# Two graph layers on one core: which PSUM banks the second layer's sums and the loaded rows' transposes use

## The chip, the cores and the metric

The kernel runs on one core of one Trainium2 chip. The metric is the device time of one execution in microseconds (us). The kernel before ran three times: 755.61, 748.73 and 752.56 us, a median of 752.56 us. One more execution was taken with the hardware profiler; it has a time and a span of its own, given below.

## The reference

There are N = 4096 nodes with D = 64 features, and a dense 4096 x 4096 adjacency matrix of zeros and ones in float32, in which a row has some eight ones on average. Two layers follow each other, both on a layer-normed and rectified input, both with a residual.

```python
# layer 0: mean over neighbours of the logarithm map on the Poincare ball
h = jnp.maximum(_layernorm(x, axis=-1), 0.0)
w = adj / jnp.maximum(adj.sum(axis=1, keepdims=True), 1e-08)
log_ij = _logmap(h[:, None, :], h[None, :, :], c)
agg = jnp.einsum('ij,ijc->ic', w, log_ij)
x = x + _expmap(0, agg @ L0_weight + L0_bias, c)
# layer 1: a row's neighbours weighted by their rank from the row's end
h = jnp.maximum(_layernorm(x, axis=-1), 0.0)
support = h @ L1_weight
rank = jnp.cumsum(mask, axis=1)
k = jnp.minimum(rank[:, -1:], 100.0)
pos = rank - (rank[:, -1:] - k)
w = mask * jnp.where(pos > 0, 0.5 ** (k - pos), 0.0)
x = x + w @ support + L1_bias
```

Layer 0 needs, for each node, the rows of its neighbours and a nonlinear function of each pair. Layer 1 is a product of a 4096 x 4096 matrix of powers of two with a 4096 x 64 matrix.

## The kernel before, in words

All is in `tile_gnn_kernel` (L549 to L1569). The nodes are cut into 32 row blocks of 128 rows; eight row blocks form a quarter, so there are four quarters, each with a mask in SBUF.

**Loads (L873 to L897).** A row block is read in two halves of 1 MB each, into one of three slots of `room`; each half is two transfers of 512 KB, issued by the sync engine SP (L879). `load(rb, h, n)` is called 128 times, n = 0 and n = 1 for each half. A call takes one PSUM bank, transposes eight 128 x 128 blocks into it on TensorE (PE, L888), and copies the bank into the quarter's mask with one instruction on ScalarE (ACT, L891). The slot is free for the next transfer when its transposes are done.

**Lists (L899 to L1130).** `pack` (PE, L917) multiplies the mask by codes, so that a row's ones become 256 words in a bank of the pool `ps_w`; `fetch_words` (ACT) copies them out, and `search` (VectorE, DVE, L981 and L983) finds the largest ones. From these come six neighbours for every row, and, per quarter, a list of the rows that have more (the tail: `tail_split`, `tail_first`, `tail_second`, whose searches are L1093 and L1095).

**Units (L1132 to L1298).** Layer 0's pairs are worked off in 17 units, numbered 0 to 16: units 0 to 15 take two row blocks each (12 gathers), units 5 to 16 have a part of the tail besides, or alone (6 or 9 gathers). `gather` (GpSimd, POOL, L1139) fetches neighbours' rows with an indirect transfer each, 288 in all. `tail_rows` prepares the tail's own rows (ACT L1156, L1163, L1170; PE L1169 and L1178), `differ` and `weigh` compute the pair's function (DVE and ACT, L1192 to L1251; L1222, L1234, L1241 and L1246 are among them), and `total` adds up: by DVE for the six, and for the tail by ACT (L1261) and PE (L1266). The gathers' buffers are two, so the gathers of unit k + 2 wait for the weights of unit k (L1234).

**The middle (L1305 to L1406).** In five groups of row blocks (8, 8, 8, 6 and 2), `middle` finishes layer 0 and makes the operand `sup` of layer 1: transposes into a bank of `ps_o` (`transposed`, L1300 to L1303), products into a bank of `ps_w` (L1333 to L1348), layer norm, and in its last stage products into `ps_t` (L1384 to L1394) and the split into three bf16 parts side by side, 192 columns (L1403, L1405).

**Layer 1's sums (L1414 to L1447).** `step` (DVE, L1412) turns a mask into layer 1's powers of two. The sum over the 32 operand blocks is cut into four parts of 16, 7, 6 and 3 blocks. `collect(c, p, n)` handles part c for two row blocks of quarter p (n = 0 to 3), so there are 64 calls: it takes one PSUM bank, fills it by matmuls (PE, L1422, 1024 in all, and L1430, 32 in the last part), and adds the bank to the result `acc`. 24 of the calls (part 0, and part 3 for n < 2) do that on DVE (L1441, L1445). The other 40 copy the bank out with ACT (L1436) into a buffer, "dg" for odd n and "mr" for even n, of which there is one each, and POOL adds the buffer's three parts to `acc` (L1438). The buffer "mr" is also what the tail's L1261 writes and L1266 reads. `write` (SP, L1451) sends finished rows out, and a flag (L1558 to L1567) ends the program.

**Who sets the order.** The functions are put in a list with the time at which each ought to run (`at`, L1454 to L1555), which becomes a priority. A scheduler then orders each engine's instructions by priority and by a timeline of its own, in which a tile has to wait until its pool has a buffer free. So the number of banks that a pool offers enters into the order written for every engine.

**The PSUM pools (L836 to L841)** hold eight banks together: `ps_a` two, `ps_w` two, and `ps_t`, `ps_o`, `ps_s` and `ps_m` one each. Before the change both `load` and `collect` take their banks from `ps_a`; `ps_w` serves `pack` and the middle's products, `ps_o` the middle's transposes.

Of the kernel before, what the change touches and what calls it, by code (L numbers as in the profile page):

```python
# [11 lines left out]
F32 = mybir.dt.float32  # L12
BF16 = mybir.dt.bfloat16
# [6 lines left out]
P = 128  # L20
# [28 lines left out]
QB = 8  # L49
# [499 lines left out]
def kernel(  # L549
# [66 lines left out]
    with ExitStack() as fast:  # L616
# [174 lines left out]
        late = masks[NQ - 1].bitcast(F32).rearrange("p b c -> p (b c)")  # L791
# [44 lines left out]
        ps_a = fast.enter_context(tc.tile_pool(name="ps_a", bufs=2, space=PSUM))  # L836
        ps_w = fast.enter_context(tc.tile_pool(name="ps_w", bufs=2, space=PSUM))
        ps_t = fast.enter_context(tc.tile_pool(name="ps_t", bufs=1, space=PSUM))
        ps_o = fast.enter_context(tc.tile_pool(name="ps_o", bufs=1, space=PSUM))
# [4 lines left out]
        st = {}  # L844
# [3 lines left out]
        sums = [(0, 16, (0, 1)), (16, 7, (2,)), (23, 6, (3,)), (29, 3, (4,))]  # L848
# [6 lines left out]
        sup, o = [], 0  # L855
        for c, (_, nb, _) in enumerate(sums):
            n = nb + (c == len(sums) - 1)
# [15 lines left out]
        def load(rb, h, n):  # L873

            k = (NH * rb + h) % LD
            a_sb = room[:, k * HC : (k + 1) * HC]
            if n == 0:
                for m in range(2):
                    nc.sync.dma_start(  # L879
                        out=a_sb[:, bass.ts(m, HC // 2)],  # L880
                        in_=adj_v[rb // JH, rb % JH, :, h * HC + m * HC // 2 : h * HC + (m + 1) * HC // 2],
                    )
            a_ps = ps_a.tile([P, QB, P], BF16, name="a_ps")

            upper = a_sb.bitcast(BF16)
            for k in range(QB):
                e = 2 * (QB * n + k) + 1
                nc.tensor.transpose(a_ps[:, k, :], upper[:, e : 2 * HC : 2 * JH], ident_b)  # L888
            q, b = divmod(rb, QB)
            j0 = h * JH + n * QB  # L890
            nc.scalar.activation(  # L891
                masks[q][:, j0 : j0 + QB, bass.ts(b, P)],
                a_ps,
                AF.Copy,
                scale=2.0**-ONE,
                saturate=False,
            )  # L897
# [515 lines left out]

        def collect(c, p, n):  # L1414

            pool = 0 < c < len(sums) - 1 or (c == len(sums) - 1 and n >= 2)
            b0, nb, _ = sums[c]
            end = c == len(sums) - 1
            o = ps_a.tile([P, 2, 2 * P], F32, name="a_ps")
            for k in range(2):  # L1420
                for j in range(nb):
                    nc.tensor.matmul(  # L1422
                        o[:, k, 0:W3],
                        lhsT=masks[p][:, b0 + j, bass.ts(2 * n + k, P)],
                        rhs=sup[c][:, j, :],
                        start=(j == 0),
                        stop=(j == nb - 1 and not end),
                    )
                if end:
                    nc.tensor.matmul(  # L1430
                        o[:, k, 0:W3], lhsT=last, rhs=sup[c][:, nb, :], start=False, stop=True
                    )
            ab = acc[:, p * QB + 2 * n : p * QB + 2 * n + 2, :]
            if pool:
                ev = (lst if n % 2 else blk).tile([P, 2, W3], F32, name="dg" if n % 2 else "mr")
                nc.scalar.activation(ev, o[:, :, 0:W3], AF.Copy, scale=2.0**-W8_SHIFT)  # L1436
                for k in range(3):
                    nc.gpsimd.tensor_tensor(ab, ab, ev[:, :, k * D : k * D + D], ALU.add)  # L1438
                return
            red = lst.tile([P, 2, D], F32, name="wsb")  # L1440
            nc.vector.tensor_reduce(  # L1441
                red, o[:, :, 0:W3].rearrange("p k (n c) -> p k c n", n=3), AX.X, ALU.add
            )
            a = ab.rearrange("p k c -> p (k c)")
            nc.vector.scalar_tensor_tensor(  # L1445
                a, red.rearrange("p k c -> p (k c)"), 2.0**-W8_SHIFT, a, ALU.mult, ALU.add
            )  # L1447
# [18 lines left out]
        for rb in range(NB):  # L1466
            for n in range(4):
                t = T0 + TLOAD * (rb + n / 4)
                at(t, load, rb, n // 2, n % 2)
                at(t + TLOAD / 4 * 1.3, pack, rb, n // 2, n % 2)  # L1470
            at(loaded(rb) + 1.0, fetch_words, rb)
            at(loaded(rb) + 2.0, search, rb)
            if rb % 2:
                at(loaded(rb) + 5.5, counts, rb - 1)
                at(loaded(rb) + 8.0, seeds, rb - 1)
                nl = 2 if rb < QB else 4
                if (rb + 1) % nl == 0:
                    at(loaded(rb) + 5.0, ell_lists, rb + 1 - nl, nl)
# [62 lines left out]
        for when, c, p in pairs:  # L1541
            t = max(t, when + 20.0)
            left[p] -= 1
            for n in range(QB // 2):
                at(t, collect, c, p, n)
                t += max(1.0, 0.2 * sums[c][1])
                if left[p] == 0 and n % 2:
                    at(t, write, p, n // 2)
# [43 lines left out]
```

## Time and profile before

| what | value |
|---|---|
| three runs | 755.61, 748.73, 752.56 us, median 752.56 us |
| profiled execution, its own time | 754.09 us |
| its span | 752.2 us |
| mean granted TensorE clock | 0.668 |
| PE busy | 400.0 us (53%) |
| DVE busy | 403.2 us (54%) |
| POOL busy | 350.5 us (47%) |
| ACT busy | 345.6 us (46%) |
| adjacency transfers (q1) | 72.93 MB, 26.9% of the time of 16 DMA engines |

The span is the profiled part of the execution; 1.9 us of its time lie outside. The profiled execution took 1.5 us more than the median of the runs.

The profile page names an instruction by its line, engine and operation, then its output and input tiles with buffer numbers left out, and a count. In a group's row the first pair of numbers is the total busy time and the mean length in ns of one instruction; the next is the idle time of that engine just before these instructions and the releaser that ended most of it. A timeline row begins with the start and the length in us and ends with the idle time ahead and its releaser. The releaser "issue" means that the profile shows nothing that the engine waited for, and "remote" that the event came from somewhere the trace does not name. In a table of windows each row gives the length of the window, then busy time and, in brackets, number of instructions of PE, PE's weight loads, DVE, ACT and POOL, then the granted clock, the busy share of the DMA engines and GB/s.

### The profile page before, as it was taken

The numbers are of one execution on the slowest core, as the hardware profiler recorded it, in microseconds if no ns is written. First come the engines' busy times: TensorE is split into PE (matmuls) and PEld (weight loads), VectorE is DVE, ScalarE is ACT, GpSimd is POOL, SyncE is SP. The second block draws the span as 40 slices with busy tenths as digits, with TensorE's granted clock in tenths as the row PEclk, the third lists the DMA queues.
The fourth block names the chain that finished last, engine by engine and source line by source line (L and its number), as shares of the span: only waits on it lengthen the run. The fifth ranks groups of instructions, "written<-read, shape, count | busy, mean of one in ns | idle before, by whom it ended". The sixth has DMA issues, their size and how long they took to land.

```text
span 752.2 us, 11841 instructions
## 1 busy us (share of the span) xinstructions
PE 400.0 (53%) x4094; PEld 344.2 (46%) x4094; DVE 403.2 (54%) x1557; ACT 345.6 (46%) x791; POOL 350.5 (47%) x423
## 2 busy tenths in 40 slices
PE   3742465643632628636067351452274378979881
PEld 3542353532531517535054241342164168979871
DVE  7742386734880518927169463793623136764520
ACT  6742465733842529836156251343242214565430
POOL 1374606246475440562705454587274713007892
PEclk9865576755855757855556555555556669988997
DMA  8994567755963536956201111221111110000001
GB/s 310 384 323 137 192 217 245 261 168 154 343 198 94 180 95 217 322 164 191 33 17 17 29 34 23 44 38 26 30 27 33 28 15 13 14 10 1 2 22 40
DMA packets 42858, 88.23 MB, mean 117 GB/s; under 512 B 14756, under 2 KB 20388, under 8 KB 42660
## 3 DMA queue, kind: packets, MB, share of 16 engines
q1 hardware_dynamic: 21458, 72.93, 26.9%
q0 software_dynamic: 9504, 10.67, 8.1%
q10 hardware_dynamic: 11826, 3.78, 2.3%
q8 instruction: 34, 0.56, 0.3%
q14 instruction: 36, 0.29, 0.1%
HBM read 83.11 MB, written 4.24 MB: 116 GB/s over the span
## 4 chain that ended last, share of the span: by engine, by line
DVE 23%; another core or an unknown queue 22%; PE 20%; ACT 16%; issue 10%; DMA 5%; ACTq 2%; POOL 1%; DVEq 0%; SPq 0%; POOLq 0%
PE a_ps L1422 9%; ACT mask L891 7%; PE a_ps L888 3%; DVE mask L1412 3%; PE words L917 2%; DMA room<-in_adj 2%; DVE cand L981 1%; DVE tl L1095 1%; DVE tb L1093 1%; ACT oh L1156 1%; PE sel L1266 1%; POOL acc L1438 1%; DVE wsb L983 1%; DMA w_sb<-in_L_gnn_weight 1%
## 5 line engine op out<-in xcount | busy, mean ns | idle before, releaser
L1139 POOL DMA_INDIRECT g<-tab_d,ell_i x192 | 198.0, 1031 | 266.2 <-DVE d L1234 84.7
L891 ACT ACTIVATE mask<-a_ps 128x1024 fp8e5<-128x1024 bf16 x128 | 128.2, 1028 | 113.8 <-remote 84.6
L888 PE MATMUL a_ps<-ident_b,room 128*128 128x128 bf16 x1024 | 107.4, 272 | 63.6 <-ACT mask L891 37.4
L1422 PE MATMUL a_ps<-room,mask 128*128 128x192 bf16 x1024 | 109.1, 260 | 32.5 <-issue 25.9
L888 PEld LDWEIGHTS <-room 128*128 128x128 bf16 x1024 | 92.9, 158 | 69.9 <-issue 68.0
L1139 POOL DMA_INDIRECT g<-tab_d,tail_i x96 | 93.8, 977 | 50.8 <-issue 28.1
L1422 PEld LDWEIGHTS <-mask 128*128 128x128 fp8e5 x1024 | 93.1, 104 | 41.1 <-issue 39.3
L917 PEld LDWEIGHTS <-mask 128*128 128x128 fp8e5 x1024 | 49.5, 115 | 107.6 <-ACT mask L891 56.7
L917 PE MATMUL words<-pk,mask 128*128 128x64 bf16 x1024 | 61.1, 219 | 70.2 <-ACT mask L891 44.4
L981 DVE MAX8 cand<-wsb 128x8 f32<-128x256 f32 x96 | 40.5, 422 | 88.5 <-ACT wsb L928 80.8
L1266 PE MATMUL sel<-d,mr 128*128 128x65 f32 x192 | 41.3, 379 | 20.2 <-issue 16.7
L1266 PEld LDWEIGHTS sel<-d,mr 128*128 128x128 f32 x192 | 39.0, 295 | 24.9 <-issue 19.6
L1438 POOL TENSOR_TENSOR acc<-acc,dg 128x128 f32<-128x128 f32 x60 | 28.2, 469 | 36.0 <-ACT dg L1436 33.9
L1412 DVE TENSOR_TENSOR mask<-mask 128x1024 int16<-128x1024 int16 x60 | 40.7, 678 | 6.6 <-ACT q__5085 L1241 4.0
L1441 DVE TENSOR_REDUCE wsb<-a_ps 128x128 f32<-128x384 f32 x24 | 13.3, 555 | 46.0 <-remote 27.8
L1261 ACT ACTIVATE mr<-oh,r 128x128 f32<-128x128 bf16 x96 | 29.3, 389 | 18.0 <-DVE acc L1445 7.5
L1438 POOL TENSOR_TENSOR acc<-acc,mr 128x128 f32<-128x128 f32 x60 | 28.5, 475 | 14.6 <-ACT mr L1436 12.7
L1169 PE MATMUL mi<-ident_b,oh 128*128 128x128 bf16 x96 | 12.6, 283 | 38.1 <-ACT oh L1163 28.2
L904 PE MATMUL words<-gn,ones_b 1*128 1x352 bf16 x32 | 12.3, 390 | 35.1 <-ACT cn L931 20.9
L1156 ACT ACTIVATE oh<-row,tail_r 128x128 bf16<-128x128 bf16 x96 | 29.4, 389 | 3.2 <-DVE tail_r L1109 3.1
L1169 PEld LDWEIGHTS <-oh 128*128 128x128 bf16 x96 | 8.9, 128 | 41.1 <-ACT oh L1163 29.2
L1170 ACT COPY mr<-mi 128x768 bf16<-128x768 bf16 (+1 forms) x20 | 13.5, 674 | 30.6 <-PE mi L1169 12.2
(332 smaller groups left out, 775.1 us busy)
## 6 DMA issues: line engine op xcount, KB each, us to landing
room<-in_adj SPq DMA_DIRECT2D x128, 512.0 KB
g<-tab_d,ell_i POOLq DMA_INDIRECT x192
hp_d<-mask SPq DMA_DIRECT2D x1, 1560.0 KB
g<-tab_d,tail_i POOLq DMA_INDIRECT x96
mr<-hp_d ACTq DMA_DIRECT2D x8, 146.2 KB
tab_d<-mask POOLq DMA_DIRECT2D x2, 520.0 KB
hi<-tab_d ACTq DMA_DIRECT2D x16, 65.0 KB
mask<-in_x SPq DMA_DIRECT2D x2, 512.0 KB
```

What stands on the lines that cost most here:

```text
L888: nc.tensor.transpose(a_ps[:, k, :], upper[:, e : 2 * HC : 2 * JH], ident_b)
L891: nc.scalar.activation(masks[q][:, j0 : j0 + QB, bass.ts(b, P)], a_ps, AF.Copy, scale=2.0**-ONE, saturate=False,)
L917: nc.tensor.matmul(w, lhsT=masks[q][:, j, bass.ts(b, P)], rhs=pk, start=False, stop=True, skip_group_check=True,)
L981: nc.vector.max(out=top, in_=src)
L1139: nc.gpsimd.indirect_dma_start(out=g[:, k, :], out_offset=None, in_=tab_d, in_offset=bass.IndirectOffsetOnAxis(ap=i, axis=0),)
L1156: nc.scalar.activation(oh[:, k, :], row128, AF.Abs, bias=tail_r[:, t0 + k // TB, k % TB : k % TB + 1], scale=-1.0,)
L1169: nc.tensor.transpose(mp[:, k - k0, :], oh[:, k, :], ident_b)
L1261: nc.scalar.activation(mr[:, k, :], u["oh"][:, k, :], AF.Copy, scale=r[:, e2 + k : e2 + k + 1])
L1266: nc.tensor.matmul(ag[:, k // TB, :], lhsT=mr[:, k, :], rhs=d[:, e2 + k, :], start=(k % TB == 0), stop=(k % TB == TB - 1),)
L1412: nc.vector.tensor_tensor(m[:, :, j, :], m[:, :, j, :], m[:, :, j - 1 if j else JH - 1, :], ALU.add)
L1422: nc.tensor.matmul(o[:, k, 0:W3], lhsT=masks[p][:, b0 + j, bass.ts(2 * n + k, P)], rhs=sup[c][:, j, :], start=(j == 0), stop=(j == nb - 1 ...
L1438: nc.gpsimd.tensor_tensor(ab, ab, ev[:, :, k * D : k * D + D], ALU.add)
```

## The change

Two functions change where their PSUM bank comes from. In `load`, every third call takes the bank of `ps_o` in place of one of `ps_a`: 86 calls take `ps_a` and 42 take `ps_o`. In `collect`, calls with odd n take a bank of `ps_w` and calls with even n one of `ps_a`. The local name `pool` of `collect` becomes `late`. The pools themselves stay as they are. No instruction is added or removed, but the order in which the scheduler writes them changes on every engine but SP.

```diff
@@ load
-            a_ps = ps_a.tile([P, QB, P], BF16, name="a_ps")
+            pool, name = (ps_a, "a_ps") if st.setdefault("loads", 0) % 3 < 2 else (ps_o, "o")
+            st["loads"] += 1
+            a_ps = pool.tile([P, QB, P], BF16, name=name)
@@ collect
-            pool = 0 < c < len(sums) - 1 or (c == len(sums) - 1 and n >= 2)
+            late = 0 < c < len(sums) - 1 or (c == len(sums) - 1 and n >= 2)
             b0, nb, _ = sums[c]
             end = c == len(sums) - 1
-            o = ps_a.tile([P, 2, 2 * P], F32, name="a_ps")
+            pool, name = (ps_w, "words") if n % 2 else (ps_a, "a_ps")
+            o = pool.tile([P, 2, 2 * P], F32, name=name)
@@ collect, further down
-            if pool:
+            if late:
                 ev = (lst if n % 2 else blk).tile([P, 2, W3], F32, name="dg" if n % 2 else "mr")
```

## The prediction

> **What bounds the kernel now.** I read the page first (shares, groups), then POOL's waits, the timelines of POOL and PE, and windows over the last 150 us. No engine is busy over 54% of the span, so the bound differs by stage. The dearest groups of the page (busy, mean ns, idle ahead and what ended it):
> ```profile
> L1139 POOL DMA_INDIRECT g<-tab_d,ell_i x192 | 198.0, 1031 | 266.2 <-DVE d L1234 84.7
> L891 ACT ACTIVATE mask<-a_ps 128x1024 fp8e5<-128x1024 bf16 x128 | 128.2, 1028 | 113.8 <-remote 84.6
> L888 PE MATMUL a_ps<-ident_b,room 128*128 128x128 bf16 x1024 | 107.4, 272 | 63.6 <-ACT mask L891 37.4
> L1139 POOL DMA_INDIRECT g<-tab_d,tail_i x96 | 93.8, 977 | 50.8 <-issue 28.1
> ```
> The 288 gathers, at some 1.25 us each with their gap, fill about 360 us of POOL between 33 and 634 us; the rest of that stretch POOL waits, mostly for a unit's weights (L1234) two units back. So up to 634 us the path runs from a unit's weights through the next gathers, with loads sharing ACT, PE and the transfer queue. After it POOL has only the L1438 additions, and its timeline shows them late and then dense (start, length):
> ```profile
> 633.14 0.95 POOL L1139 DMA_INDIRECT g<-tab_d,tail_i  x1 [0.30 <-issue]
> 666.70 1.52 POOL L1438 TENSOR_TENSOR acc<-acc,dg 128x128 f32<-128x128 f32 x3 [32.60 <-ACT dg L1436]
> 678.05 1.83 POOL L1438 TENSOR_TENSOR acc<-acc,mr 128x128 f32<-128x128 f32 x3 [9.84 <-ACT mr L1436]
> 680.48 1.72 POOL L1438 TENSOR_TENSOR acc<-acc,mr 128x128 f32<-128x128 f32 x2 [0.60 <-ACT mr L1436]
> 682.16 0.45 POOL L1438 TENSOR_TENSOR acc<-acc,dg 128x128 f32<-128x128 f32 x1
> ```
> From 682 to 739 us POOL hardly pauses, and 13 us of output follow. The windows (PE busy comes first, POOL's fifth) say who is full before and after that point:
> ```profile
> 634.00:648.00 14.00, 13.30 (x146) 12.55 (x145) 12.46 (x43) 9.19 (x26) 0.09 (x1) 0.88 0.08 19
> 648.00:662.00 14.00, 14.00 (x155) 13.39 (x151) 10.44 (x31) 8.66 (x28) 0.00 (x0) 1.00 0.01 2
> 662.00:678.00 16.00, 11.23 (x110) 10.37 (x109) 9.12 (x51) 9.95 (x32) 1.36 (x3) 0.85 0.04 11
> 678.00:694.00 16.00, 15.95 (x149) 15.03 (x148) 7.57 (x18) 7.64 (x19) 13.76 (x29) 0.83 0.01 2
> ```
> PE is full until 662 us, then POOL and PE both have a hole until 678 us. There PE's next sum waits for a bank whose evacuation (L1436) stands behind the last unit's chain on ACT, because the evacuation into "mr" needs the buffer which the unit's L1266 frees at 677.5 us. A third view, PE's timeline while POOL gathers, shows single matmuls that wait for nothing the profile names:
> ```profile
> 597.34 0.32 PE L1422 MATMUL a_ps<-room,mask 128*128 128x192 bf16 x1 [1.79 <-issue]
> 599.46 0.32 PE L1422 MATMUL a_ps<-room,mask 128*128 128x192 bf16 x1 [1.80 <-issue]
> 601.57 0.32 PE L1422 MATMUL a_ps<-room,mask 128*128 128x192 bf16 x1 [1.79 <-issue]
> ```
> More banks cannot help a PE that crawls like this. ACT likewise stood still for 20.4 us up to 277.1 us, inside a gather.
>
> **What the Trainium skill says.** "Perfetto Trace Analysis", Optimization Strategy: consistent bubbles can mean too little SBUF or PSUM for the next tile. The trace agrees only in the stretch 662 to 678 us; before it PE has no bubble, after it POOL is the busy one. "PSUM — Partial Sum Buffer", Specifications (TRN2): eight banks to a partition, and GpSimd reaches none. That is this kernel's shape: its pools hold all eight banks, and each late sum needs a copy by ACT (0.49 us) before POOL adds. The same page, Engine vs sequencer instructions: the queues of ScalarE, VectorE and GpSimd are strict FIFO. The trace agrees: the evacuations at 677.5 us stand behind L1261 at 674.2 us. So a bank freed later by ACT order is not cured by one more bank. "Perfetto Trace Analysis", DMA Instruction — SWDGE (GPSIMD): the row ends when descriptors are written, not when data landed; so the 0.95 us of a gather is POOL's own work, which no bank shortens.
>
> **The change part by part.** No instruction is added or removed: 1024 transposes (L888), 1024 matmuls (L1422), 128 mask copies, 40 evacuations and 120 additions stay. Of the 128 loads, 42 now use the bank "o", which the middle's own transposes (L1302) use too; of the 64 sums 32 use the two "words" banks, which L917 (packing) and L1345 (middle) use. What is moved is the order that the scheduler writes out, because it models banks; I compared the two programs engine by engine.
>
> *The tail.* In the new program the sums with odd n of the second group (six of them) stand ahead of the last unit's chain on ACT and PE, and all go through the buffer "dg". Each costs 0.49 us (copy) and about 1.5 us (three additions) in series, near 2.0 us; the hole of 9.84 us takes five. At 682.3 us POOL would have seven tiles done where it had 3.3: 3.7 tiles at 1.42 us (what a tile with alternating buffers takes in the dense stretch) is 5.2 us gained. What is late next: those same buffers. The rest of the group now ends in a run of five "mr" tiles and has one more "mr" pair, five pairs in one buffer, where an addition waits for a copy of 0.49 us plus hand-over, about 0.6 us each (the 0.60 in the timeline): 3.0 us lost. The dense stretch has 3.7 us of small gaps that end with an evacuation; with four banks about 1.5 us of it goes. Sum: -5.2 + 3.0 - 1.5 = -3.7 us. Bounds: 0 (the six evacuations each wait for POOL, and L1241, L1246 and L1261 of the last unit queue behind them on ACT, so the unit ends later) and -7. The last sums' operands are ready 8 to 10 us before they are used, so this much fits.
>
> *The middle of the units.* In the new program seven pairs of tail searches (L1093, L1095) stand on DVE ahead of unit 11's weights, and on PE 43 more matmuls of the first group (65 for 22), and their wait for a words bank, ahead of unit 13's tail rows (L1169). Gather 13 began without a wait at 507.1 us; unit 11's weights were at 500.95 us, so 6 us were spare. Seven pairs are about 6 us of DVE plus a transfer's round trip; two evacuations of the first group (L1441, 0.56 us each) now stand ahead of unit 13's weights, the gate of gather 15. With half of the 6 us hidden in the slack I take +3 us. Bounds 0 and +7.
>
> *The loads.* A third bank lets PE transpose one more load while ACT stalls. The scheduler used it to pull loads forward: ahead of unit 5's L1222 on ACT stand 99 mask copies for 90, of unit 6's 118 for 105, from unit 8 on 128 for 128. Each is 1.03 us of ACT and 0.5 MB of transfer, 1.5 us at the 346 GB/s seen from 307 to 324 us. That work has to be done anyway; in before, 11 of these 13 ran in the shadow of gather 8. If the new order only fills earlier holes (ACT idles 113.8 us ahead of L891) nothing is lost; I take +1 us. Bounds -10 and +17.
>
> Sum against the profiled execution (754.1 us: span 752.2, about 1.9 around it): -3.7 + 3 + 1 = +0.3 us. The profiled execution lies 1.5 us above the median of the runs; carried over to the median of 752.6 this is 752.9 us.
>
> **The rivals.** *Likeliest: about the same, 752.9 us* (746 to 758). For: after 678 us POOL limits, before 662 us PE is full, and the gathers' length is untouched.
>
> *Faster, 743 us.* The third bank really is what loads lack: PE waits 37.4 us at L888 for L891, and SP's load transfers wait 118.5 us for L888. At each of some eight ACT stalls one more half slot is freed, 8 x 1.5 = 12 us of transfer; half on the path, 6, and the tail's 3.7: -9.7 us. Against: behind the transposes the mask still needs ACT, and the longest stall, 15.5 us, would still be there one load later.
>
> *Slower, 763 us.* One mechanism: unit 6's weights, the gate of gather 8 at 307.3 us, are put behind 13 more loads (17 us), and gather 8 then runs with nothing left to hide. If half of it is not won back later (8 us) and the middle costs its upper 7 us, less the tail's 3.7: +11. It decides from the point where gather 8 starts over 8 us later and the last gather (634 us) does too.
>
> *No effect on the banks' waits, 757 us.* The words banks are held by the middle's L1345 until its copy L1353, so PE stands at the fourth sum of the first group ahead of unit 13's tail rows: +4 us with the tail's gain used up by the last unit's later chain.
>
> **How the numbers follow.** Likeliest 0.36, faster 0.21, slower 0.35, the last 0.08. About 1% is what a measurement here can tell from no change, so 745 to 760 us is "same": the likeliest and the last, 0.44 in all, faster 0.20, slower 0.36, the edges of the cases trading a point. The range reaches over the middle of both outer cases: 743 less 2 for a tail of its full -7, 741; 763 plus 5 for more of the 17 us not won back, 768. The faster case beyond 741 and the slower one beyond 768 leave out about 0.2.
>
> **What would show it.** Tail right: five "dg" additions between 668 and 678 us, and POOL dense to the end some 4 us earlier counted from the last gather; wrong: the last unit's L1261 later by as much. Middle: gather 13 with a wait ahead of it, ended by DVE L1234. Loads: start of gather 8 against 307.3 us, and ACT's wait at L891. The forecast is wrong if the last gather ends more than 8 us away from 634 us in either direction, since nothing behind it makes that good.

## The result, and the profile after

The changed kernel took 785.3 us (780.81 to 788.81, four runs) against 752.69 us before (the three runs and a fourth of 752.83 us): 1.043 of before, 95% interval 1.036 to 1.051, or 32.6 us more. The forecast was 752.9 us, its upper end 768.

The run of the changed kernel that was profiled has a span of 782.7 us, 30.5 us longer. In the changed source the lines after `load` stand two further down, those after `collect` three (L1141 was L1139, L1236 was L1234, L1441 was L1438). The same groups on its page:

```profile
L1141 POOL DMA_INDIRECT g<-tab_d,ell_i x192 | 193.7, 1009 | 304.4 <-DVE d L1236 94.3
L893 ACT ACTIVATE mask<-a_ps 128x1024 fp8e5<-128x1024 bf16 x86 | 86.8, 1034 | 95.0 <-remote 71.4
...
L1141 POOL DMA_INDIRECT g<-tab_d,tail_i x96 | 91.9, 958 | 50.3 <-issue 27.7
...
L890 PE MATMUL a_ps<-ident_b,room 128*128 128x128 bf16 x688 | 71.7, 272 | 30.1 <-ACT mask L893 10.5
```

A gather still costs 1.0 us; PE's wait for a transposing bank fell as intended, from 37.4 to 10.5 us for the two banks of `ps_a`. But the idle time ahead of the neighbours' gathers rose from 266.2 to 304.4 us. POOL's timeline at the end, to be laid beside that of before, whose last addition is the first line here:

```profile
738.00 0.98 POOL L1438 TENSOR_TENSOR acc<-acc,dg 128x128 f32<-128x128 f32 x2
```
```profile
664.96 0.95 POOL L1141 DMA_INDIRECT g<-tab_d,tail_i  x1 [0.31 <-issue]
697.97 2.13 POOL L1441 TENSOR_TENSOR acc<-acc,dg 128x128 f32<-128x128 f32 x3 [32.07 <-ACT dg L1439]
700.70 1.53 POOL L1441 TENSOR_TENSOR acc<-acc,dg 128x128 f32<-128x128 f32 x3 [0.60 <-ACT dg L1439]
702.83 1.54 POOL L1441 TENSOR_TENSOR acc<-acc,dg 128x128 f32<-128x128 f32 x3 [0.60 <-ACT dg L1439]
...
725.54 1.58 POOL L1441 TENSOR_TENSOR acc<-acc,mr 128x128 f32<-128x128 f32 x3 [1.04 <-ACT mr L1439]
729.52 1.52 POOL L1441 TENSOR_TENSOR acc<-acc,mr 128x128 f32<-128x128 f32 x3 [2.40 <-ACT mr L1439]
732.98 1.53 POOL L1441 TENSOR_TENSOR acc<-acc,mr 128x128 f32<-128x128 f32 x3 [1.94 <-ACT mr L1439]
736.76 0.99 POOL L1441 TENSOR_TENSOR acc<-acc,dg 128x128 f32<-128x128 f32 x2 [2.25 <-ACT dg L1439]
...
769.30 0.99 POOL L1441 TENSOR_TENSOR acc<-acc,mr 128x128 f32<-128x128 f32 x2
```

The last gather starts at 664.96 instead of 633.14 us, 31.8 us later. The hole of 9.84 us is filled with "dg" tiles as forecast, and what was won there is lost again further on, mostly in the run of "mr" tiles. From the first addition to the end of the last (770.28 us here, 738.98 before) both kernels take 72.3 us. So the whole loss lies ahead of the last gather. Where, is read from the starts of the gathers (us, from the two timelines of POOL):

| gathers of unit | 3 | 4 | 5 | 6 | 7 | 8 | 10 | 12 | 13 | 14 | 16 |
|---|---|---|---|---|---|---|---|---|---|---|---|
| before | 116.7 | 145.8 | 170.5 | 197.2 | 251.5 | 307.3 | 401.6 | 476.3 | 507.1 | 543.3 | 626.8 |
| after | 119.5 | 151.3 | 180.6 | 214.3 | 277.6 | 331.6 | 424.4 | 503.7 | 540.3 | 572.9 | 658.7 |
| later by | 2.8 | 5.5 | 10.1 | 17.1 | 26.1 | 24.3 | 22.8 | 27.4 | 33.2 | 29.6 | 31.9 |

26.1 us are lost by unit 7. The gathers of units 5, 6 and 7 wait for the weights of units 3, 4 and 5, so 20.6 us of them (26.1 less 5.5) are lost while units 3 to 5 are worked off. Only 3.3 us are won back by unit 10, and from there to unit 16 another 9.1 us are lost, 5.8 of them at unit 13. Four timelines of the changed kernel show the dearest piece, between unit 6's gathers and unit 7's; first ACT, then PE, then DVE, then POOL:

```profile
223.44 1.15 ACT L1165 ACTIVATE oh<-oh 128x1152 bf16<-128x1152 bf16 x1
229.25 1.02 ACT L893 ACTIVATE mask<-o 128x1024 fp8e5<-128x1024 bf16 x1 [4.65 <-remote]
241.86 1.02 ACT L893 ACTIVATE mask<-a_ps 128x1024 fp8e5<-128x1024 bf16 x1 [11.60 <-remote]
255.89 0.80 ACT L1172 COPY mr<-mi 128x768 bf16<-128x768 bf16 x1 [13.00 <-remote]
...
274.36 1.35 ACT L1224 ACTIVATE g<-d 128x1344 f32<-128x1344 f32 x1
```
```profile
230.32 1.01 PE L890 MATMUL o<-ident_b,room 128*128 128x128 bf16 x8 [3.99 <-issue]
256.74 0.48 PE L1171 MATMUL mi<-ident_b,oh 128*128 128x128 bf16 x3 [25.41 <-ACT mr L1172]
...
259.71 0.70 PE L1180 MATMUL mi<-mr 128*128 128x65 bf16 x9
```
```profile
261.34 0.43 DVE L983 MAX8 cand<-wsb 128x8 f32<-128x256 f32 x1 [21.13 <-ACT wsb L930]
...
271.57 0.35 DVE L1210 TENSOR_TENSOR d<-g,mi 128x192 f32<-128x192 f32 x1
```
```profile
277.56 0.94 POOL L1141 DMA_INDIRECT g<-tab_d,ell_i  x1 [24.98 <-DVE u L1237]
```

The same places in the kernel before:

```profile
241.81 1.02 ACT L891 ACTIVATE mask<-a_ps 128x1024 fp8e5<-128x1024 bf16 x1 [6.23 <-remote]
...
248.34 1.32 ACT L1222 ACTIVATE g<-d 128x1344 f32<-128x1344 f32 x1
```
```profile
243.31 0.68 PE L1178 MATMUL mi<-mr 128*128 128x65 bf16 x9 [1.25 <-ACT mr L1170]
```
```profile
246.81 0.34 DVE L1208 TENSOR_TENSOR d<-g,mi 128x192 f32<-128x192 f32 x1
```
```profile
251.52 0.95 POOL L1139 DMA_INDIRECT g<-tab_d,ell_i  x1 [12.96 <-DVE u L1235]
```

While POOL gathers (up to 252.6 us), ACT does one instruction in some 12 us and PE waits for it. In both kernels ACT runs freely again 3.3 us after the gathers' end, at 255.89 us here and at 241.81 us before. From there to unit 5's L1224 it needs 18.5 us, with eleven mask copies of loads on the way; before, to L1222, it needed 6.5 us, with four. The copies do not hold L1224 by themselves. L1224 squares what DVE's L1210 writes, and L1210's last input comes from PE's L1180, which had ended at 260.4 us. But L1210 ran only at 271.57 us, 11.2 us later, since nine searches (L983), with the rest of the list work of loads pulled ahead, are written in front of it on DVE; before, it ran 2.8 us after its input, behind three searches. That is 8.4 of the 12.0 us. The copies are in it too, since the first of the nine waits for words that ACT copies out behind some of them (L930, 5.0 us after ACT runs freely, where before it was 1.3 us). So unit 5's weights, and with them the gathers of unit 7, wait for loads and their lists that the scheduler now puts ahead.

Why is this not won back later, when fewer loads are left? The windows from unit 8's gathers to unit 9's, first before, then after (PE, weight loads, DVE, ACT, POOL, clock, DMA share, GB/s):

```profile
307.30:335.50 28.20, 14.82 (x135) 13.44 (x133) 15.70 (x52) 16.66 (x33) 22.09 (x21) 0.63 0.74 256
335.50:350.70 15.20, 6.90 (x73) 6.48 (x72) 12.18 (x51) 9.88 (x15) 0.04 (x2) 0.61 0.66 218
```
```profile
331.60:358.80 27.20, 9.80 (x66) 8.96 (x66) 12.04 (x55) 13.13 (x28) 21.04 (x21) 0.52 0.44 136
358.80:374.60 15.80, 2.98 (x37) 2.28 (x38) 11.92 (x49) 3.51 (x8) 0.00 (x0) 0.50 0.11 19
```

ACT has 16.6 us of work here in place of 26.5, PE 12.8 in place of 21.7, and the stretch is as long as before: 43.0 us for 43.4. In its first part POOL gathers; in its second DVE is the fullest engine and has as much to do as before, 11.9 us for 12.2. The loads were free in it. Moved ahead of units 3 to 6, they are paid for.

### The profile page after: what moved, and what is told of

It reads as the page before. It is cut to its first block, busy times and chain, and to the rows that moved or that the text cites. A ratio compares the mean times of both kernels' runs of the same rounds, so it can differ in the third digit from the quotient of the medians.

```text
span 782.7 us, 11824 instructions
## 1 busy us (share of the span) xinstructions
PE 407.9 (52%) x4094; PEld 347.3 (44%) x4094; DVE 409.7 (52%) x1557; ACT 344.2 (44%) x791; POOL 344.4 (44%) x423
## 4 chain that ended last, share of the span: by engine, by line
another core or an unknown queue 26%; DVE 23%; PE 18%; ACT 12%; issue 8%; DMA 5%; POOL 4%; ACTq 1%; SPq 0%; DVEq 0%; POOLq 0%
ACT mask L893 5%; POOL acc L1441 4%; PE words L1425 4%; PE a_ps L1425 4%; DVE mask L1414 4%; DMA room<-in_adj 3%; PE a_ps L890 2%; DVE tl L1097 2%; DVE tb L1095 2%; DVE cand L983 1%; PE sel L1268 1%; PE o L890 1%; DMA w_sb<-in_L_gnn_weight 1%; ACT mr L1263 1%
## 5 line engine op out<-in xcount | busy, mean ns | idle before, releaser
L1141 POOL DMA_INDIRECT g<-tab_d,ell_i x192 | 193.7, 1009 | 304.4 <-DVE d L1236 94.3
L893 ACT ACTIVATE mask<-a_ps 128x1024 fp8e5<-128x1024 bf16 x86 | 86.8, 1034 | 95.0 <-remote 71.4
L1425 PEld LDWEIGHTS <-mask 128*128 128x128 fp8e5 x1024 | 96.8, 107 | 50.1 <-issue 47.1
L890 PEld LDWEIGHTS <-room 128*128 128x128 bf16 x1024 | 91.3, 158 | 52.9 <-issue 52.6
L1141 POOL DMA_INDIRECT g<-tab_d,tail_i x96 | 91.9, 958 | 50.3 <-issue 27.7
L919 PEld LDWEIGHTS <-mask 128*128 128x128 fp8e5 x1024 | 48.3, 114 | 119.3 <-ACT mask L893 59.9
L983 DVE MAX8 cand<-wsb 128x8 f32<-128x256 f32 x96 | 40.2, 419 | 110.2 <-ACT wsb L930 88.9
L890 PE MATMUL a_ps<-ident_b,room 128*128 128x128 bf16 x688 | 71.7, 272 | 30.1 <-ACT mask L893 10.5
L1425 PE MATMUL a_ps<-room,mask 128*128 128x192 bf16 x512 | 62.4, 271 | 17.8 <-issue 14.5
L1425 PE MATMUL words<-room,mask 128*128 128x192 bf16 x512 | 60.9, 264 | 20.2 <-issue 17.4
L1268 PE MATMUL sel<-d,mr 128*128 128x65 f32 x192 | 38.5, 364 | 40.6 <-issue 21.3
L1268 PEld LDWEIGHTS sel<-d,mr 128*128 128x128 f32 x192 | 36.7, 283 | 42.7 <-issue 22.9
L893 ACT ACTIVATE mask<-o 128x1024 fp8e5<-128x1024 bf16 x42 | 43.5, 1035 | 16.7 <-remote 11.8
L1441 POOL TENSOR_TENSOR acc<-acc,dg 128x128 f32<-128x128 f32 x60 | 28.6, 477 | 41.0 <-ACT dg L1439 38.2
L890 PE MATMUL o<-ident_b,room 128*128 128x128 bf16 x336 | 37.6, 266 | 14.4 <-issue 11.1
L906 PE MATMUL words<-gn,ones_b 1*128 1x352 bf16 x32 | 12.1, 383 | 43.7 <-ACT cn L933 40.2
```

The lines of the kernel that those rows point to most:

```text
L893: nc.scalar.activation(masks[q][:, j0 : j0 + QB, bass.ts(b, P)], a_ps, AF.Copy, scale=2.0**-ONE, saturate=False,)
L919: nc.tensor.matmul(w, lhsT=masks[q][:, j, bass.ts(b, P)], rhs=pk, start=False, stop=True, skip_group_check=True,)
L983: nc.vector.max(out=top, in_=src)
L1141: nc.gpsimd.indirect_dma_start(out=g[:, k, :], out_offset=None, in_=tab_d, in_offset=bass.IndirectOffsetOnAxis(ap=i, axis=0),)
L1268: nc.tensor.matmul(ag[:, k // TB, :], lhsT=mr[:, k, :], rhs=d[:, e2 + k, :], start=(k % TB == 0), stop=(k % TB == TB - 1),)
L1425: nc.tensor.matmul(o[:, k, 0:W3], lhsT=masks[p][:, b0 + j, bass.ts(2 * n + k, P)], rhs=sup[c][:, j, :], start=(j == 0), stop=(j == nb - 1 ...
```

## The experiments

**How to compare.** In the five groups of runs the kernel before took between 566 and 767 us. The record names chip 7 for the first, third and fourth group, where it took 766.9, 748.8 and 764.7 us, chip 12 for the second and chip 11 for the fifth. So each ratio is to the kernel before in the same group, and absolute times are not compared between groups; the times in the expectations of the first group were meant for a kernel before of 753 us. The experiments' sources keep the line numbers of the kernel before. Theory 1: the third transposing bank makes the scheduler write loads and searches ahead of the units' steps, and the gathers wait. Theory 2: the bank itself does it, letting transposes and transfers run into the gathers. Theory 3: the sums' use of the "words" banks.

**First group: the parts, and the order without the bank** (before 766.88 us). In `e1_load` only `load` is changed, in `e2_sums` only the bank line of `collect`. In `e3_push` no bank is changed; this is the part of the line `EARLY` that differs:

```diff
-"tail_rows":30,"differ":30,"weigh":30,"total":30,"total_tail":30
+"tail_rows":20,"differ":20,"weigh":20,"total":20,"total_tail":20
```

In `e4_from56` the third bank is there, but only from the 57th load call on (one line there, three here):

```diff
-a_ps = ps_a.tile([P, QB, P], BF16, name="a_ps")
+pool, name = (ps_a, "a_ps") if st.setdefault("loads", 0) % 3 < 2 or st["loads"] < 56 else (ps_o, "o")
+st["loads"] += 1
+a_ps = pool.tile([P, QB, P], BF16, name=name)
```

> Only the third transposing bank of the change; the sums keep the two banks of ps_a. The scheduler writes the same order up to unit 10 as for the whole change: 66, 80, 99 and 118 mask copies on ACT ahead of units 3 to 6, for 62, 72, 90 and 105 before. Theory 1 (the third bank makes the scheduler put loads and searches ahead of the units' weights, and the gathers wait for these): nearly the whole loss, 775 to 786 us, gather 7 starting near 277 us for 251 before. Theory 3 (the sums' use of the words banks costs): within 1% of before, 745 to 760 us.

> Only the sums' four banks of the change; loads keep two banks. The order of loads, searches and units is that of before; only matmuls of the sums move. Theory 1: 746 to 757 us, the gathers starting as before. Theory 3: 775 us or more, the loss coming after gather 11.

> Two transposing banks as before, but the units' own steps get a lead of 20 us in place of 30 in the planner, so that loads and searches come ahead of them: 66, 76, 94 and 112 mask copies ahead of units 3 to 6. Theory 1 (order): slower by roughly half of the change's loss, 760 to 775 us, with gathers 5 to 8 later. Theory 2 (the third bank itself, by letting transposes and transfers run ahead into the gathers): as before, 748 to 757 us.

> Three transposing banks, but only from the 57th load call on; sums as before. The written order up to unit 5 is nearly that of before (62, 72, 91 mask copies ahead of units 3 to 5; 111 ahead of unit 6 for 105). Theory 1 (order): 750 to 764 us, gathers 5 to 7 starting within 4 us of before. Theory 2 (the bank itself): the loads from 57 to 100 run in the stretch where the loss arose, so gather 7 is 10 us or more later and the time is 768 us or more.

Measured, as ratios to before with the 95% interval: `e1_load` 1.029 (1.024 to 1.034), `e2_sums` 0.996 (0.993 to 0.999), `e3_push` 1.024 (1.019 to 1.029), `e4_from56` 1.011 (1.004 to 1.017). Theory 3 falls: the sums alone lose nothing. `e1_load` is slower by 22.8 us of medians, more than two thirds of the change's 32.6 us; the whole change was not run in this group. The start of unit 7's gathers, POOL's timeline, in that order of the four kernels:

```profile
284.56 0.95 POOL L1139 DMA_INDIRECT g<-tab_d,ell_i  x1 [28.72 <-DVE u L1235]
```
```profile
261.12 0.94 POOL L1139 DMA_INDIRECT g<-tab_d,ell_i  x1 [14.30 <-DVE u L1235]
```
```profile
273.44 1.00 POOL L1139 DMA_INDIRECT g<-tab_d,ell_i  x1 [23.32 <-DVE d L1234]
```
```profile
261.07 0.94 POOL L1139 DMA_INDIRECT g<-tab_d,ell_i  x1 [12.52 <-DVE u L1235]
```

With two banks and the order pushed, unit 7 is 12.3 us late; with three banks and the order kept, not at all (261.07 beside 261.12; `e2_sums`, which has the order of before, stands in for it). That speaks for theory 1 and against theory 2. What `e4_from56` loses, it loses later: its gathers of unit 13 wait 9.2 us.

**Second group: undo the order, keep the banks** (before 566.36 us). `e5_after` is the change itself. `e6_held` is the change with loads put back in the planner:

```diff
-EARLY = {"middle":30, ...
+EARLY = {"load":-10,"pack":-10,"middle":30, ...
```

`e7_one` has the sums' four banks and, from the 41st load call on, one transposing bank (`ps_o`). `e8_upto56` has the third bank up to the 56th load call only (`or st["loads"] >= 56` in the condition).

> The change as it is, once more, for a comparison on this chip with the other three and with the kernel before. Both theories: 1.03 to 1.05 of before, gather 7 some 25 us later than where the order is that of before.

> The whole change, all three transposing banks and the sums' four, but the planner gives load and pack a priority 10 us later, so the scheduler writes the units nearly where they were: 62, 73, 91 and 112 mask copies on ACT ahead of units 3 to 6 (before 62, 72, 90, 105; the change 66, 80, 99, 118). Theory 1 (order): gather 7 within 4 us of before, most of the loss gone, ratio to before 0.998 to 1.014; what is left comes after gather 7 (unit 6, and the tail searches ahead of unit 11). Theory 2 (the third bank itself): still 1.03 or more.

> The other direction: sums in four banks, loads in two banks up to the 40th call and in the one bank of ps_o from then on. The scheduler then writes fewer loads ahead of the units: 56, 62, 79, 89, 106 and 117 mask copies ahead of units 3 to 8. Theory 1 (order): gather 7 starts 8 to 20 us earlier than before; at the end 0.975 to 1.00 of before, as later gathers then carry the loads. Theory 2 (banks limit the loads): the loads starve, 1.01 or more.

> Three transposing banks only up to the 56th load call, two after it; sums as before. The order is pushed although the bank is not there any more when the loss arises: 66, 79, 97 and 114 mask copies ahead of units 3 to 6. Theory 1 (order): gather 7 is 16 to 25 us later than in the order of before, ratio 1.02 to 1.035. Theory 2 (the bank itself): at most 1.012, since loads 57 to 100 run with two banks.

Measured: `e5_after` 1.005 (1.002 to 1.009), `e6_held` 1.001 (0.998 to 1.005), `e7_one` 1.034 (1.023 to 1.045), `e8_upto56` 1.003 (1.000 to 1.006). Here the loss is nearly gone for the change itself: `e5_after` missed what both theories had forecast, `e8_upto56` and `e7_one` what theory 1 had, and `e6_held` tells nothing apart. `e7_one` came out as theory 2 had it, 1.01 or more, and shows a limit to theory 1: fewer loads ahead of the units is not always better; with one bank it was 3.4% slower. `e8_upto56` too lies where theory 2 put it, but where the change itself costs 0.5% this decides nothing. What differs on this chip is shown by ACT's waits up to 345 us, for the change in its first trace and here:

```profile
ACT mask L893 <- remote: 79.1, 12, 13.4
ACT mask L893 <- PE o L890: 13.6, 8, 7.5
ACT mask L893 <- PE a_ps L890: 13.4, 11, 2.2
ACT mr L1172 <- remote: 13.0, 1, 13.0
```
```profile
ACT mask L891 <- PE a_ps L888: 11.6, 14, 1.7
ACT g L1222 <- DVE d L1192: 10.1, 2, 7.9
ACT g L1222 <- DMA g<-tab_d,tail_i: 8.7, 2, 6.7
ACT wsb L928 <- DVE cand L981: 8.5, 6, 5.8
```

The waits for "remote", in which ACT stands still while POOL gathers, are absent. Yet the pushed order delays unit 7 here too; only, it is won back. The gathers of units 7 and 10 in `e5_after` and then in `e6_held`:

```profile
207.25 1.03 POOL L1139 DMA_INDIRECT g<-tab_d,ell_i  x1 [0.32 <-DVE u L1235]
...
297.36 0.94 POOL L1139 DMA_INDIRECT g<-tab_d,ell_i  x1 [2.36 <-DVE d L1234]
```
```profile
194.16 0.94 POOL L1139 DMA_INDIRECT g<-tab_d,ell_i  x1 [0.30 <-DVE u L1235]
...
293.78 0.94 POOL L1139 DMA_INDIRECT g<-tab_d,ell_i  x1 [2.08 <-DVE w L1198]
```

The delay is 13.1 us at unit 7 and 3.6 us at unit 10. That the missing standstills are what lets it be won back is likely, but not shown.

**Third group: the same where before takes about 750 us again** (before 748.84 us).

> The held version again (the whole change, load and pack 10 us later in the planner), because the kernel before took 566 us where it ran first and 753 to 767 us where the loss was seen. Theory 1 (order, and engines that stand still while POOL gathers make it dear): where before takes 740 us or more, 0.998 to 1.016 of it, gather 7 within 4 us of the kernel before; where before takes about 566 us, within 0.5% of it. Theory 2 (the third bank itself): 1.03 or more where before takes 740 us or more.

> The change again. Both theories: 1.035 to 1.05 where before takes 740 us or more, about 1.005 where it takes some 566 us.

> Third transposing bank only up to the 56th load, order pushed, again. Theory 1: 1.02 to 1.035 where before takes 740 us or more, gather 7 16 to 25 us later; about 1.003 where it takes some 566 us. Theory 2: at most 1.012 everywhere.

> The kernel before itself, for its trace on this chip. Where it takes about 566 us, the waits of ACT ahead of L891 during gathers (20.4 us up to 277 us in the first trace) should be gone, and POOL should run from gather to gather with 0.3 us between; where it takes 740 us or more, the gathers start as in the first trace, within 3% of the time.

Measured: `f1_held` 1.022 (1.018 to 1.027), `f2_after` 1.041 (1.036 to 1.046), `f3_upto56` 1.035 (1.031 to 1.039), `f4_before` 744.63 us in its one run. Unit 7's gathers for `f4_before`, `f1_held`, `f2_after`, `f3_upto56`:

```profile
256.50 0.94 POOL L1139 DMA_INDIRECT g<-tab_d,ell_i  x1 [13.90 <-DVE u L1235]
```
```profile
256.63 0.95 POOL L1139 DMA_INDIRECT g<-tab_d,ell_i  x1 [11.26 <-DVE u L1235]
```
```profile
278.87 0.94 POOL L1139 DMA_INDIRECT g<-tab_d,ell_i  x1 [28.19 <-DVE u L1235]
```
```profile
273.78 0.95 POOL L1139 DMA_INDIRECT g<-tab_d,ell_i  x1 [24.27 <-DVE u L1235]
```

With all banks of the change and the order put back, unit 7 starts 0.1 us from before; with the third bank gone after the 56th load but the order still pushed, it is 17.3 us late. Theory 2 had `f3_upto56` at 1.012 at most and `f1_held` at 1.03 or more; both came out on the other side. Over the first and third group the delay grows with the mask copies that stand ahead of unit 5, each against the kernel of the same group with 90: 91 copies (`e4_from56`, `f1_held`) 0.0 and 0.1 us, 94 (`e3_push`) 12.3, 97 (`f3_upto56`) 17.3, 99 (`f2_after`, `e1_load`) 22.4 and 23.4 us. From 94 on this is 2.5 to 3.1 us for each copy above 90. It is no fixed price: in the second group `e5_after` (99 copies) was 13.1 us behind `e6_held` (91), 1.6 us for each. The copies count what moved; how much of the delay their transposes, packing and searches carry was not tried one by one. Theory 1 holds for the early part. But `f1_held` missed its range: 2.2% stay, and they come after unit 11.

**Fourth and fifth group: what stays** (before 764.68 and 763.46 us). Two accounts of the 2.2% were tried. M1: seven more tail searches stand on DVE ahead of unit 11's weights (43 for 36). M2: the sums in four banks stand ahead of units 13 and 14. `g1_both_held` is `f1_held` with `"tail_second":30` made -20; `g2_load_held` is `e1_load` with the edit of `e6_held`; `g3_two_held` is the kernel before with that edit alone; `g4_sums` is `e2_sums` again. `h1_both_held` and `h2_two_held` repeat `g1_both_held` and `g3_two_held`.

> All banks of the change. Load and pack 10 us later in the planner, and the last tail search (tail_second) 50 us later, so that 36 of the L1093 stand ahead of unit 11's weights as before (43 in the change), and 62, 74, 93, 112 mask copies ahead of units 3 to 6. If what is left after gather 10 is the seven searches ahead of unit 11 (M1): 0.993 to 1.010 of before where before takes 740 us or more. If it is the sums that stand ahead of units 13 and 14 in four banks (M2): 1.015 or more.

> Only the loads' third bank, load and pack 10 us later in the planner; sums in two banks as before. 43 of the L1093 ahead of unit 11. M1: 1.013 to 1.027, the loss coming between gathers 11 and 14. M2: at most 1.008.

> The kernel before with all its banks (loads two, sums two) and one edit: load and pack 10 us later in the planner. 62, 72, 89, 106 mask copies ahead of units 3 to 6, as before, but 43 of the L1093 ahead of unit 11. M1: 1.010 to 1.025, with no bank changed at all. M2, or theory 2 (the third bank itself): at most 1.005.

> Only the sums' four banks, again, beside the other three. M1: 0.990 to 1.002. M2: 1.010 or more.

> All banks of the change, loads held and the seven searches behind unit 11's weights, again, in case the chip is one on which before takes about 750 us: there the held version with the searches in front lost 2.2%. M1: 0.995 to 1.010, gather 13 without a wait. M2: 1.015 or more. Where before takes about 765 us: 1.000 to 1.007 as in the first run.

> No bank changed, load and pack 10 us later in the planner, the seven searches ahead of unit 11's weights, again. M1: where before takes about 750 us, 1.010 to 1.025, gather 13 with a wait of some 9 us and gather 14 late too; where before takes about 765 us, 0.997 to 1.004 as in the first run, since gather 14 wins the delay back there. M2: at most 1.005 everywhere.

Measured: `g1_both_held` 1.004 (1.001 to 1.007), `g2_load_held` 1.006 (1.002 to 1.010), `g3_two_held` 1.001 (0.997 to 1.004), `g4_sums` 0.999 (0.995 to 1.003); `h2_two_held` 1.004 (1.002 to 1.007), and `h1_both_held` has a median of 767.0 us in four runs, too few for an interval. By whole times M2 fails (`g1_both_held` and `g4_sums` lose nothing like 1%), and M1 fails for `g2_load_held` and `g3_two_held`, which lose 0.6% at most. Of the gathers, those of units 13 and 14 in `g3_two_held` (searches in front, no bank changed) and then in `g1_both_held` (searches behind, all banks):

```profile
526.17 0.94 POOL L1139 DMA_INDIRECT g<-tab_d,ell_i  x1 [9.27 <-DVE w L1198]
...
558.79 0.94 POOL L1139 DMA_INDIRECT g<-tab_d,ell_i  x1 [9.55 <-DVE u L1235]
```
```profile
518.80 0.95 POOL L1139 DMA_INDIRECT g<-tab_d,ell_i  x1 [0.30 <-issue]
...
558.28 0.95 POOL L1139 DMA_INDIRECT g<-tab_d,ell_i  x1 [16.78 <-DVE u L1235]
```

The searches cost unit 13 its start without a wait, 7.4 us, and unit 14 waits 7.2 us less: won back here. The same is seen across the traces outside the second group: with 43 searches ahead of unit 11's weights the gathers of unit 13 wait 7.6 to 10.3 us in all ten, whatever the banks; with 36 they wait 0.3 us in five of six (`e2_sums`, the exception, 6.2). In the third group the delay was not won back: `f1_held` was 10.1 us late at unit 13 and 17.1 us at unit 14, where `f4_before` did not wait at all. Which of the two happens seems to hang on whether unit 14's gathers wait in the kernel before (13.8 us in its first trace, none in `f4_before`); in no later group did the kernel before take near 750 us, though the fourth ran on chip 7 again, so the cause of these last 16 us is not settled.

## Why the prediction was wrong

**The loads: the failed step.** I took +1 us with bounds -10 and +17 for the loads pulled ahead of the units, because that work has to be done anyway. Up to unit 7 it measured +26.1 us, and +22.8 by unit 10, outside the bounds. Two errors made it. The first is the price of a load: I counted its copy on ACT (1.03 us) and its transfer (1.5 us) and put the searches that come with it on DVE at nothing. In the dearest piece unit 5 waits for these: L1210 ran 11.2 us after its input, where it had been 2.8 us. In all, the delay came to 2.5 to 3.1 us for each copy above 90. (The 17 us that I wrote for 13 loads follow from neither price: 13 copies are 13.4 us, 13 transfers 19.5.) The second is that I reckoned with fewer loads later giving time back, where the windows show the later stretch as long as before with 10 us less of ACT's work in it. I had seen ACT stand still for 20.4 us in a gather and did not ask what it means for work written ahead of a unit: the time between the gathers is then nearly all there is for it.

**The place.** The slower rival had the mechanism, units behind loads, but at unit 6 and gather 8, with half won back, at 763 us. The time is lost at units 3 to 5, where the counts I had written down (99 for 90 ahead of unit 5) already were; 3.3 of 26.1 us are won back by unit 10. What it named as deciding came true, gather 8 24.3 us late and the last gather 31.8. The range ended at 768 since I halved what I could not place.

**The middle.** +3 us, bounds 0 and +7: from unit 7 to unit 16 the delay grew from 26.1 to 31.9 us, 5.8 us. That is within the bounds only because 3.3 us were won back first; from unit 10 on it grew by 9.1, outside them. Gather 13 waits as forecast (7.64 us; the releaser named is L1198, L1200 here, which stands right behind L1234 on DVE), and it alone adds 5.8 us. Its working, six us of searches ahead of unit 11, is shown by `g3_two_held` against `g1_both_held` (7.4 us at unit 13); that it lasts to the end is not, as it was won back there.

**The tail.** -3.7 us, bounds 0 and -7: 0.0 us. The "dg" tiles came into the hole, and POOL had its seven tiles done where I put them, 15 us after the first. The term that was too small is the run of "mr" tiles: I took 0.6 us for each of five pairs, 3.0 us in all. The four waits inside the run are 0.60, 1.04, 2.40 and 1.94, the "dg" tile behind it waits another 2.25, and the fifth pair waits 0.60 as I took it: 8.8 us. The 3.7 us of small gaps went altogether, where I took 1.5. So -5.2 + 8.8 - 3.7 is -0.1 us, an estimate that meets the measured zero: that the total stayed within its bounds is two errors that cancel.

**What was right.** The faster rival's premise, that PE's wait for a transposing bank falls, came true (L890 on L893, 37.4 to 10.5 us for `ps_a`) and gained nothing: PE's waits for ACT at other places rose, at L906 (before L904) from 20.9 to 40.2 us. The length of a gather and the output at the end hardly moved (13.3 us of output before, 12.4 after). The strict FIFO queues of ScalarE, VectorE and GpSimd, which the Trainium skill states in "PSUM — Partial Sum Buffer", Engine vs sequencer instructions, are what the early loss rests on too, and the trace agrees: L1210, ready at 260.4 us, ran at 271.57 us, behind nine searches.

Nothing that was run beats both kernels for sure: the sums' four banks alone gave 0.996 (0.993 to 0.999) once and 0.999 (0.995 to 1.003) once, and the medians of all runs in those two groups are 766.68 against 766.88 us and 764.65 against 764.68 us.

## What to carry to other kernels

Where a scheduler orders the instructions, a buffer more is an edit of the order: compare the two orders first, count what now stands ahead of the instruction that the critical engine waits for, and price it with all that comes along, not with its own row. Ask also whether that work was free where it stood: moved out of a shadow, it is paid for, and the emptied shadow need not pay it back. Here it gave back 3.3 of 26.1 us; where ACT did not stand still, 9.5 of 13.1. To tell a buffer's effect from that of its order, put the order back by priorities and keep the buffer, and push the order without the buffer.

## What the runs showed of the hardware

The kernel before took 752.7, 766.9, 566.4, 748.8, 764.7 and 763.5 us (medians, in the order of the groups, the first result ahead), the same program every time. The record names chip 7 for the second, fourth and fifth of these, chip 12 for the third and chip 11 for the last, and none for the first. So on one chip number the medians differ by 2.4% between groups, and chip 12 was 24% below the lowest of the others. On chip 12 ACT had none of the waits for "remote" that made 79.1 us at its mask copies up to 345 us in the first trace of the change, and the same change cost 0.5% there in place of 4.1 to 4.3%. While POOL's gathers are issued, ACT stands still, its releaser unnamed in the trace, in some of the groups and not in another; what holds it there, no run here shows.
